# A re-planned attention stage: half as many border copies on GpSimd, one copy tied behind a matmul, and a new order on every engine

## The chip, the cores and the metric

The kernel runs as one program on one core of a Trainium2 chip. A core has five engines, each of which works through its own queue of instructions in order: TensorE (PE in the profile; its weight loads are PEld), VectorE (DVE), ScalarE (ACT), GpSimd (POOL) and SyncE (SP, which here only issues DMAs). An instruction starts when the one before it on its engine has started or ended and when the semaphores that it names have been raised by other engines or by DMAs.

The metric is the device time of one execution in microseconds (us), the median of several runs.

## The reference, cut to what matters

The input is `x` of shape (2, 256, 48, 48): two images (b) of 256 channels. The reference has two layers. Only the first is touched by the change. After a group norm, layer 0 computes a 7x7 local attention with reflected borders and a branch of nine depthwise convolutions, and adds both to the input:

```python
q = (_c1x1(x, Wq, bq) * HD ** (-0.5)).reshape(b * HEAD, HD, n)
k = _c1x1(x, Wk, bk);  v = _c1x1(x, Wv, bv)            # 1x1 convolutions, 4 heads of 64
uk  = _unfold(jnp.pad(k, rpad, mode='reflect'), KA)     # 49 neighbours of each pixel
uv  = _unfold(jnp.pad(v, rpad, mode='reflect'), KA)
upe = _unfold(jnp.pad(pe, rpad[1:], mode='reflect'), KA)
att = softmax(einsum('bdn,bdkn->bnk', q, uk + upe))
out_att = einsum('bnk,bdkn->bdn', att, uv)
...
out_conv = jnp.sum(oc * wts, axis=1)                    # depthwise branch
return rate1 * out_att + rate2 * out_conv
```

Layer 1 (a state space block with a scan, then a mixture of eight experts, two per token) takes the result. Its program is the same before and after.

## The kernel before, in words

The program is three stages, one after the other: layer 0 (to about 315 us of the profile), the state space block (to about 700 us) and the experts (to the end).

**How layer 0 is tiled.** Each image is cut into 18 blocks of 8x16 queries (three blocks make a row of blocks), 36 in all, numbered c = 0 to 35. A block looks at 14x22 = 308 keys. For block c the steps are, with the names that the planner gives them:

- `score` (PE, L810): eight matmuls, queries by keys, for two pairs of heads; into two of three double PSUM banks (`banks`).
- `least` (DVE, L826): mask, and the maximum of each row; `exps` (ACT, L837): exponentials and their sums; `turn` (PE, L845): six transpositions; `copy` (ACT, L851): the transposed probabilities back to SBUF. Each of these exists twice per block, for h = 0 and 1.
- `rden` (DVE, L883): the inverses of the sums; `rx` (POOL, L888): each inverse widened to 64 columns; `rt` (PE, L893): two transpositions that spread the inverses over the output's layout, into the right half of a PSUM bank called `o`; `rc` (ACT, L899): that half copied to SBUF (`rb`).
- `mix` (PE, L867): 24 matmuls, values by probabilities, into the left half of the same bank `o`; `norm` (DVE, L881): left half times `rb`; `add` (DVE, L877): into `x`.

Around the blocks stand steps that serve several of them. `kk` (PE, L702), `ka` (DVE, L708) and `kb` (POOL, L713 to L722) make the keys, in five groups of ten rows (the last of eight) for each image and each h. `kb` mirrors the borders: for j = 0, 1, 2 one column on the left (L715) and one on the right (L717), and in the first and last group three whole rows (L720, L722). `place` (POOL, L691) makes the position term that `ka` adds. `qp` and `q` (PE L659, ACT L667) make the queries of a row of blocks. `v`, `vc`, `vs` (PE L748, ACT L755, a DMA from SP, L758) make the values in 18 pieces; after every three pieces `vt` (SP, L768 to L774, nine DMAs) spreads them into a table in HBM, `ve` (L780, L782) mirrors its ends, and `val` (L910, three DMAs) loads a block's 308 rows of it. The convolution branch is `c1`, `c2`, `c3` on DVE (L565, L577, L603), `cp`, `g2`, `relu` on ACT (L626, L597, L569), and `ca` on POOL (L638), which issues a DMA that adds a product into a sum; `cd` stands for its landing. Lastly there are the statistics of each image (`gs`, `ga`, `rstd`, `xp`), and `winw`, `woutw`, ... which scale weights for layer 1.

**What sets the order.** None of this is written in the order in which it is issued. Every step is declared with an engine, a cost in nanoseconds, what it needs, and what buffers it takes and frees (`op`, class `Flow`). `Flow.run` then plays the declared costs forward: of the steps that are ready, the one with the lowest rank is emitted next on its engine. The rank is a due time (block number times `PACE0`) less the work that still hangs on the step, less an offset for the step's kind from the table `LEAD0`, which has one entry for the first image (`-`) and one for the second (`+`). The emitted order is fixed on PE, DVE, ACT and SP, and chained on POOL. So a changed cost, an added need or a new table reorders the stage on all engines; the chip still waits only on real data and buffers. DMA queues are not modelled as busy: a DMA has only a time from issue to landing.

The buffers that matter: two single PSUM banks (`bank`: shared by `kk`, `qp`, `v` and `o`), three double banks, two `vout`, two `ct`, two `place`, three `val`.

Of the kernel before, what the change touches and what calls it, by code (L numbers as in the profile page):

```python
# [34 lines left out]
ALU = mybir.AluOpType  # L35
# [3 lines left out]
B, C, H, W = 2, 256, 48, 48  # L39
# [3 lines left out]
PAD = 3  # L43
# [189 lines left out]
class Kernel:  # L233
# [133 lines left out]
    def prepare(self, wts):  # L367

        nc, ins, v, r = self.nc, self.ins, self.v, self.r
        l0 = self.l0 = {}  # L370

        def new(name, *shape):
            l0[name] = wts.tile([P, *shape], F32, name=name)
            return l0[name]

        wp = wts.tile([1, 2, P], F32, name="wp")
        pos = wts.tile([1, 2, HP], F32, name="pos")
        line = self.line = wts.tile([P, 2, W], F32, name="line")
        nc.scalar.dma_start(wp, ins["Wp"])
        nc.scalar.dma_start(pos, ins["pos"])  # L380
        for k in ("Wk", "Wq", "Wv"):
            nc.scalar.dma_start(new(k, NH, C), ins[k].rearrange("(h p) o -> p h o", p=P))
        for key, cost in (("cst", 10300), ("vec", 11600), ("row", 14500), ("wp", 9900), ("Wk", 11500), ("Wq", 13500),
                          ("Wv", 15400), ("win", 24200)):
            self.arrival((key, 0), cost)
        vec = nc.vector

        self.op(0, ("bq8", 0), "DVE", 170, lambda: vec.tensor_scalar(
            new("bq8", NH), v["bq"], -(HD ** -0.5), None, ALU.mult), ("vec", 0))
        self.op(0, ("bkp", 0), "DVE", 220, lambda: vec.tensor_scalar(  # L390
            new("bkp", NH), v["bk"], v["bp"], None, ALU.add), ("vec", 0))
        self.op(0, ("w2r", 0), "DVE", 240, lambda: vec.tensor_scalar(
            new("w2r", NH * 9), v["w2"], r["rate2"], None, ALU.mult), ("vec", 0), ("row", 0))

        self.op(0, ("bv1", 0), "DVE", 220, lambda: vec.tensor_scalar(
            new("bv1", NH), v["bv"], r["rate1"], None, ALU.mult), ("vec", 0), ("row", 0))
        self.op(0, ("wv1", 0), "POOL", 1600, lambda: nc.gpsimd.tensor_scalar(
            l0["Wv"], l0["Wv"], r["rate1"], None, ALU.mult), ("row", 0), ("Wv", 0))


        def lines():
            ps = self.bank_for(("line", 0))
            for i in range(2):
                nc.tensor.matmul(
                    ps[:, i * W : (i + 1) * W], lhsT=wp[:, i, :], rhs=pos[:, i, PAD : PAD + W], start=True, stop=True
                )

        self.chain(0, ("line", 0), [
            ("PE", 450, lines),
            ("DVE", 250, lambda: vec.tensor_copy(  # L410
                line.rearrange("p i c -> p (i c)"), self.tiles["bank", ("line", 0)][:, : 2 * W])),
        ], ("wp", 0), takes=[("bank", ("line", 0))], uses=[("bank", ("line", 0))])
# [265 lines left out]
    def keys(self, b, g):  # L678


        nc, l0, T = self.nc, self.l0, self.tiles
        r0, r1 = KG * g, min(KG * (g + 1), H)
        n = (r1 - r0) * W

        c = b * NBQ + NCB * next(rb for rb in range(NRB) if min(QR * rb + QR + PAD, H) > r0)
        old = NCB * (min(NRB - 1, (r1 + PAD - 1 + (PAD if r1 == H else 0)) // QR) + 1) - 1
        rows = slice(PAD + r0, PAD + r1)
# [4 lines left out]
                t, bcast(self.line[:, 0, :], 1, shape), bcast(self.line[:, 1, r0:r1], 2, shape), ALU.add  # L692
            )

        self.op(c, ("place", (b, g)), "POOL", 1100, place, ("line", 0), takes=[("place", (b, g))])
        for h in range(NH):
            key, kp = (b, g, h), self.kp[h]

            def product(h=h, key=key):
                ps = self.bank_for(("kp", key))  # L700
                for k in range(NH):
                    nc.tensor.matmul(  # L702
                        ps[:, :n], lhsT=l0["Wk"][:, k, h * P : (h + 1) * P], rhs=self.xp[b, k][:, r0:r1, :],
                        start=k == 0, stop=k == NH - 1,
                    )

            def add(h=h, key=key, kp=kp):
                nc.vector.scalar_tensor_tensor(  # L708
                    kp[:, rows, PAD : PAD + W], T["bank", ("kp", key)][:, :n].rearrange("p (r c) -> p r c", c=W),
                    l0["bkp"][:, h : h + 1], T["place", (b, g)][:, : r1 - r0, :], ALU.add, ALU.add,  # L710
                )

            def border(kp=kp):  # L713
                for j in range(PAD):
                    nc.gpsimd.tensor_copy(kp[:, rows, j : j + 1], kp[:, rows, 2 * PAD - j : 2 * PAD - j + 1])  # L715
                    lo, hi = PAD + W + j, PAD + W - 2 - j
                    nc.gpsimd.tensor_copy(kp[:, rows, lo : lo + 1], kp[:, rows, hi : hi + 1])  # L717
                for j in range(PAD):
                    if r0 == 0:
                        nc.gpsimd.tensor_copy(kp[:, j, :], kp[:, 2 * PAD - j, :])  # L720
                    if r1 == H:
                        nc.gpsimd.tensor_copy(kp[:, PAD + H + j, :], kp[:, PAD + H - 2 - j, :])  # L722

            self.op(c, ("kk", key), "PE", 4 * 403 * n // 480, product, *self.normalized(b, r0, r1), ("Wk", 0),
                    takes=[("bank", ("kp", key))])
            self.op(c, ("ka", key), "DVE", 700 * n // 480, add, ("kk", key), ("bkp", 0), ("place", (b, g)),
                    *[("score", i) for i in range(old + 1) if b],
                    uses=[("bank", ("kp", key)), ("place", (b, g))])
            self.op(c, ("kb", key), "POOL", 6 * 170 + (3 * 180 if r0 == 0 or r1 == H else 0), border, ("ka", key),
                    ("kb", (b, g - 1, h)) if r1 == H else None)  # L730

    def values(self, b, pair):


        nc, T, p0 = self.nc, self.tiles, 2 * P * pair
        flat = [self.xp[b, h].rearrange("p r c -> p (r c)") for h in range(NH)]
        raster, key = self.vraster[b], (b, pair)
        r1 = (p0 + 2 * P) // W
        done = (p0 + 2 * P) % (VR * W) == 0
        group = p0 // (VR * W)  # L740
        c = b * NBQ + NCB * next(rb for rb in range(NRB) if min(QR * rb + QR + PAD, H) > group * VR)
# [41 lines left out]

        self.op(c, ("v", key), "PE", 1730, product, *self.normalized(b, p0 // W, r1), ("wv1", 0), takes=[("bank", ("v", key))])
        self.op(c, ("vc", key), "ACT", 570, copy, ("v", key), takes=[("vout", key)], uses=[("bank", ("v", key))])
        self.op(c, ("vs", key), "queue", 3700, store, ("vc", key), uses=[("vout", key)])
        if done:
            self.op(c, ("vt", (b, group)), "queue", 10000, spread, *[("vs", (b, p)) for p in range(pair - 2, pair + 1)])
            if group == 0 or r1 == H:
# [2 lines left out]
    def block(self, c):  # L792
# [97 lines left out]
        def spread():  # L890
# [7 lines left out]
        self.op(c, ("rt", c), "PE", 220, spread, ("rx", c), takes=[("bank", ("o", c))], uses=[("rx", c)])  # L898
        self.op(c, ("rc", c), "ACT", 390, lambda: nc.scalar.copy(  # L899
            self.large_tile("rb", c, [P, NH, P]), T["bank", ("o", c)][:, NH * P :].rearrange("p (h q) -> p h q", h=NH)  # L900
        ), ("rt", c), takes=[("rb", c)])
        self.op(c, ("norm", c), "DVE", 430, scale, ("rc", c), ("mix", c), takes=[("ot", c)],
                uses=[("bank", ("o", c)), ("rb", c)])
        self.op(c, ("add", c), "DVE", 390, add, ("norm", c), uses=[("ot", c)])
# [10 lines left out]

    PACE0 = 8517
    LEAD0 = {
        "Wk-": -1119547, "Wq-": -597473, "Wv-": 2514686, "add+": 3062471, "add-": 216523,
        "bkp-": -1357788, "bq8-": -2582335, "bv1-": -2311329, "c1+": -3056772, "c1-": 674391,
        "c2+": -3354012, "c2-": -3259309, "c3+": -4311438, "c3-": -482232, "ca+": 1060332,  # L920
        "ca-": 1695604, "cd+": -4992161, "cd-": 505317, "copy+": 3167330, "copy-": -2132730,
        "cp+": -1186244, "cp-": 185922, "cst-": 1816816, "exps+": -3784293, "exps-": -3837034,
        "g2+": 2518476, "g2-": -2098506, "ga-": -5969754, "gneg-": 1972109, "gs-": -3837384,
        "ka+": -379377, "ka-": 4594388, "kb+": 501331, "kb-": 862328, "kk+": -256854, "kk-":
        105073, "least+": -254337, "least-": -2329953, "line-": -3571457, "mix+": 1625800,
        "mix-": 4892365, "norm+": -2011005, "norm-": -1379637, "place+": 2695259, "place-":
        2798256, "q+": 1131741, "q-": 1346874, "qp+": -260479, "qp-": 44331, "rc+": 1359143,
        "rc-": 555924, "rden+": -3086582, "rden-": -738391, "relu+": 6028778, "relu-": 3311002,
        "row-": -4935504, "rstd-": 5049209, "rt+": -224859, "rt-": -1455, "rx+": -5316670,
        "rx-": -171551, "score+": 2256235, "score-": 1081046, "sw+": -1345634, "turn+": -412799,  # L930
        "turn-": 8318, "v+": 84496, "v-": 32028, "val+": 867987, "val-": 3076092, "vc+": 135346,
        "vc-": -180221, "ve+": 793092, "ve-": -4814757, "vec-": -3443444, "vs+": -1096720,
        "vs-": -3047869, "vt+": 3933614, "vt-": 2501367, "w2r-": -6504385, "win-": 1754314,
        "winw+": -1105244, "woutc+": 705933, "woutd+": 1232417, "woute+": -3991134, "woutt+":
        -1769115, "woutw+": -5095299, "wp-": -2490457, "wv1-": -892855, "x-": -4043795, "xp-":
        -7196893,
    }


# [1485 lines left out]
```

## Time and profile before

| | us |
|---|---|
| runs | 1278.13, 1283.33, 1290.38 |
| median | 1283.33 |
| profiled execution: its own time | 1286.65 |
| its span in the profile | 1284.9 |
| mean granted TensorE clock | 0.979 |
| layer 0: last `add` (DVE, L877) ends | 314.7 |

The span is the stretch from the first to the last instruction of the profiled execution; the device time has 1.75 us around it. In rows of groups, "x" is the number of instructions, then follow busy time and the mean duration of one in ns. A row of waits reads: who waited, for whom, us in total, times, longest. A row of the timeline reads: start, duration, engine, line, operation, and in brackets the idle time ahead of it and what ended it. A row of windows has a stretch's length, then busy time and number of instructions for PE, PEld, DVE, ACT and POOL, the granted clock (1.00 is full speed), and DMA.

### The profile page before, as it was taken

The page shows a single profiled execution, that of the slowest core. Times are in us where ns is not written, and L with a number is a line of the kernel's source. Part 1 is how long each engine was busy: PE and PEld are TensorE (multiplying, and loading weights), DVE is VectorE, ACT ScalarE, POOL GpSimd, SP SyncE. Part 2 cuts the span into 40 slices and gives each one's busy share as a digit, 9 for nine tenths or more (in the row PEclk, how much of TensorE's full clock was granted, in tenths as well). Part 3 has the DMA queues.
Part 4 walks back from the last instruction along what each step waited for, and adds up shares of the span by engine and source line. Part 5 has one row for each costly group of instructions (what it writes and reads, how often), then busy time and mean ns, then how long its engine had stood idle before and what let it go on. Part 6 is the DMA issues. An engine that isn't in the chain of part 4 may idle for free. (4 is left out here: it accounts for less than half of the span.)

```text
span 1284.9 us, 23472 instructions
## 1 busy us (share of the span) xinstructions
PE 1212.2 (94%) x8024; PEld 980.1 (76%) x8024; DVE 895.6 (70%) x2385; ACT 779.3 (61%) x1774; POOL 624.2 (49%) x833
## 2 busy tenths in 40 slices
PE   4889898997899999999999988999999999999995
PEld 2557775776576777777776877999999999999994
DVE  6787897998577977889798644664655565556542
ACT  2479886987889978789697643333333333333342
POOL 4654253523267789999989873112222222212220
PEclk9899998999799999999999998999999999999998
DMA  7598783632223334334545149567667567666756
GB/s 259 137 215 210 187 197 75 149 91 67 70 80 94 89 116 127 112 114 133 176 142 176 58 133 284 178 196 235 229 195 250 179 217 221 234 182 206 229 179 210
DMA packets 106734, 212.99 MB, mean 166 GB/s; under 512 B 11615, under 2 KB 83632, under 8 KB 101680
## 3 DMA queue, kind: packets, MB, share of 16 engines
q1 hardware_dynamic: 85488, 168.51, 38.9%
q0 software_dynamic: 19008, 38.62, 15.8%
q10 hardware_dynamic: 2116, 4.33, 1.0%
q8 instruction: 65, 1.06, 0.3%
q14 instruction: 57, 0.47, 0.1%
HBM read 154.24 MB, written 43.23 MB: 154 GB/s over the span
## 5 line engine op out<-in xcount | busy, mean ns | idle before, releaser
L2153 POOL DMA_INDIRECT acc<-ey,token x70 | 109.3, 1561 | 367.7 <-ACT ey L2152 308.4
L2143 PE MATMUL bank<-ext,wt 128*128 128x256 f32 (+1 forms) x1152 | 241.2, 368 | 0.0
L2147 ACT ACTIVATE hid<-bank,bt 128x256 f32<-128x256 f32 (+1 forms) x288 | 132.0, 460 | 171.3 <-PE bank L2143 166.9
L2143 PEld LDWEIGHTS bank<-ext,wt 128*128 128x128 f32 x1152 | 207.0, 190 | 25.0
L2186 PE MATMUL po<-ts,ss 128*128 128x128 f32 x768 | 96.2, 275 | 0.0
L974 PE MATMUL bank<-xn,win 128*128 128x387 f32 x240 | 92.4, 508 | 2.1 <-ACT t L1057 2.1
L1187 DVE SCALAR_TENSOR_TENSOR xc<-bank,vec,xc 128x384 f32<-128x384 f32 x144 | 86.7, 610 | 8.4 <-ACT xc L1176 8.1
L2186 PEld LDWEIGHTS po<-ts,ss 128*128 128x128 f32 x768 | 90.9, 192 | 0.0
L1403 ACT ACTIVATE mt<-mt,cum 128x128 f32<-128x128 f32 x288 | 87.7, 393 | 0.0
L1737 POOL DMA_INDIRECT xs<-u,rows x72 | 73.2, 1016 | 17.5 <-issue 14.9
L837 ACT ACTIVATE prob<-prob,top 128x308 f32<-128x308 f32 x144 | 78.4, 554 | 1.2 <-DVE top L826 1.2
L2190 ACT COPY u<-po 128x128 f32<-128x128 f32 x32 | 8.5, 265 | 114.0 <-PE po L2186 114.0
L888 POOL COPY rx<-rden 128x256 f32<-128x256 f32 x36 | 36.2, 1049 | 74.1 <-DVE rden L883 56.3
L974 PE MATMUL zbank<-xn,win 128*128 128x384 f32 x192 | 72.0, 497 | 0.0
L1509 PE MATMUL bank<-wout,y 128*128 128x264 f32 x288 | 71.8, 395 | 0.1
L2130 DVE TENSOR_TENSOR ss<-hid 128x512 f32<-128x512 f32 x32 | 22.1, 691 | 70.6 <-ACT hid L2147 70.6
L565 DVE SCALAR_TENSOR_TENSOR hid<-xp,vec,hid 128x1175 f32<-128x1175 f32 (+1 forms) x48 | 69.5, 1452 | 1.0 <-DMA hid<-ct 1.0
L826 DVE CUSTOM_DVE_ANT_0 prob<-banks,cst 128x308 f32<-128x308 f32 x144 | 62.1, 471 | 9.5 <-PE banks L810 9.2
L577 DVE SCALAR_TENSOR_TENSOR x<-hid,w2r,x 128x1128 f32<-128x1128 f32 (+1 forms) x48 | 66.0, 1383 | 0.1
L2186 PE MATMUL po<-wt,hid 128*128 128x128 f32 x496 | 65.5, 275 | 0.0
L845 PE MATMUL banks<-cst,prob 128*112 128x128 f32 x432 | 57.7, 276 | 6.0 <-ACT pt L851 3.9
L1509 PEld LDWEIGHTS bank<-wout,y 128*128 128x128 f32 x288 | 53.7, 194 | 10.1 <-issue 1.1
(340 smaller groups left out, 3015.8 us busy)
## 6 DMA issues: line engine op xcount, KB each, us to landing
wt<-in_We SPq DMA_DIRECT2D x36, 2048.0 KB
mt<-decays SPq DMA_DIRECT2D x36, 512.0 KB
ex<-xs SPq DMA_DIRECT2D x36, 265.0 KB
rd<-decays SPq DMA_DIRECT2D x68, 128.0 KB
val<-vtab SPq DMA_DIRECT2D x72, 112.0 KB
bt<-in_We SPq DMA_DIRECT2D x36, 136.0 KB
hid<-ct POOLq DMA_DIRECT2D x8, 600.0 KB
vraster<-vout SPq DMA_DIRECT2D x18, 256.0 KB
```

What stands on the lines that cost most here:

```text
L565: nc.vector.scalar_tensor_tensor(dst, src, w[:, k : k + 1], dst, ALU.mult, ALU.add)
L577: nc.vector.scalar_tensor_tensor(dst, src, w[:, k : k + 1], dst, ALU.mult, ALU.add)
L837: nc.scalar.activation(t, t, AF.Exp, bias=T["top", c][:, a : a + 1], scale=-1.0, accum_out=T["den", c][:, a : a + 1])
L974: self.nc.tensor.matmul(ps, lhsT=lhs(k), rhs=rhs(k), start=k == 0, stop=k == NH - 1)
L1187: nc.vector.scalar_tensor_tensor(out(), T["bank", ("cv", at)][:, i : i + TB], wc[:, i : i + 1], out(), ALU.mult, ALU.add)
L1403: nc.scalar.activation(t, t, AF.Relu, bias=at_s, scale=-1.0)
L1509: nc.tensor.matmul(ps[:, : C + E], lhsT=T["y", c][:, m, :], rhs=self.l1["wout"][:, m, :], start=m == 0, stop=m == NZ - 1,)
L1737: ins = nc.gpsimd.indirect_dma_start(self.xs, bass.IndirectOffsetOnAxis(ap=of("rows")[:, i, q : q + 1], axis=0), T["u2", g][:, i, :], None,)
L2143: nc.tensor.matmul(ps[:, :rows], lhsT=w1[:, k, c * P : (c + 1) * P], rhs=xt[:, k, :], start=k == 0, stop=k == NH - 1,)
L2147: nc.scalar.activation(hid[:, c, :], ps[:, :rows], AF.Gelu, bias=bt[:, c : c + 1])
L2153: put = nc.gpsimd.indirect_dma_start(self.acc, bass.IndirectOffsetOnAxis(ap=token[:, j : j + 1], axis=0), y, None, compute_op=ALU.add)
L2186: nc.tensor.matmul(p[name], lhsT=v[a][:, c], rhs=v[w][:, c], start=c == 0, stop=c == NHC // 2 - 1)
```

## The change

Five edits, all in layer 0's declarations:

1. `kb` mirrors the left and the right column of one j in one operation with a step of 51 (to) and 43 (from) between the two columns, instead of two operations. Three column operations per `kb` instead of six; there are 20 `kb`.
2. `rc` needs `mix` of its block as well as `rt`.
3. `wv1` (POOL, the value weights times `rate1`) needs `rstd` of the first image.
4. Declared costs: `place` 1260 for 1100, `kb` 1350 (+1200 with rows) for 1020 (+540), `kk` of the first image's first two groups 560 per matmul for 403, `vs` 4500 for 3700.
5. A new table `LEAD0` (all 91 offsets).

```diff
         self.op(0, ("wv1", 0), "POOL", 1600, ...
-            l0["Wv"], l0["Wv"], r["rate1"], None, ALU.mult), ("row", 0), ("Wv", 0))
+            l0["Wv"], l0["Wv"], r["rate1"], None, ALU.mult), ("row", 0), ("Wv", 0), ("rstd", 0))
...
-        self.op(c, ("place", (b, g)), "POOL", 1100, place, ...
+        self.op(c, ("place", (b, g)), "POOL", 1260, place, ...
...
             def border(kp=kp):
                 for j in range(PAD):
-                    nc.gpsimd.tensor_copy(kp[:, rows, j : j + 1], kp[:, rows, 2 * PAD - j : 2 * PAD - j + 1])
-                    lo, hi = PAD + W + j, PAD + W - 2 - j
-                    nc.gpsimd.tensor_copy(kp[:, rows, lo : lo + 1], kp[:, rows, hi : hi + 1])
+                    to, of = PAD + W, W - 2 - PAD
+                    nc.gpsimd.tensor_copy(
+                        kp[:, rows, j : j + to + 1 : to], kp[:, rows, 2 * PAD - j : 2 * PAD - j + of + 1 : of]
+                    )
...
-            self.op(c, ("kk", key), "PE", 4 * 403 * n // 480, product, ...
+            self.op(c, ("kk", key), "PE", 4 * (403 if b or g > 1 else 560) * n // 480, product, ...
-            self.op(c, ("kb", key), "POOL", 6 * 170 + (3 * 180 if r0 == 0 or r1 == H else 0), border, ...
+            self.op(c, ("kb", key), "POOL", 3 * 450 + (3 * 400 if r0 == 0 or r1 == H else 0), border, ...
...
-        self.op(c, ("vs", key), "queue", 3700, store, ...
+        self.op(c, ("vs", key), "queue", 4500, store, ...
...
         self.op(c, ("rc", c), "ACT", 390, ...
-        ), ("rt", c), takes=[("rb", c)])
+        ), ("rt", c), ("mix", c), takes=[("rb", c)])
...
     LEAD0 = {
-        "Wk-": -1119547, "Wq-": -597473, "Wv-": 2514686, "add+": 3062471, "add-": 216523,
+        "Wk-": -2983844, "Wq-": -2364428, "Wv-": 1379269, "add+": 4672699, "add-": -218998,
...
```

What the new order is, as the built programs have it: on PE, both `kk` of the fourth key group move ahead of the first queries, and the second row's queries (`qp`) move from before the second and third `score` to behind the third; the second image's statistics (`rstd`) move up to just behind the first `score`. On DVE, that image's statistics and `xp` likewise move up. On POOL, the four `winw` and four `woutw` move up among the first blocks, and for the second image `rx` 16 and 17 move ahead of most of the `kb`. On SP, the second `vt` moves from behind the first three `val` to ahead of them, and the second image's value pieces come earlier. From block 18 on the two orders differ mostly by a place or two. Every step of the state space block and the experts is emitted in the same order as before.

More of the change, by code (lines that the diff above doesn't have):

```diff
@@ L693, in place @@
             )
-        self.op(c, ("place", (b, g)), "POOL", 1100, place, ("line", 0), takes=[("place", (b, g))])
+        self.op(c, ("place", (b, g)), "POOL", 1260, place, ("line", 0), takes=[("place", (b, g))])
         for h in range(NH):
@@ L722, in border @@
                         nc.gpsimd.tensor_copy(kp[:, PAD + H + j, :], kp[:, PAD + H - 2 - j, :])
-            self.op(c, ("kk", key), "PE", 4 * 403 * n // 480, product, *self.normalized(b, r0, r1), ("Wk", 0),
+            self.op(c, ("kk", key), "PE", 4 * (403 if b or g > 1 else 560) * n // 480, product, *self.normalized(b, r0, r1), ("Wk", 0),
                     takes=[("bank", ("kp", key))])
@@ L728, in keys @@
                     uses=[("bank", ("kp", key)), ("place", (b, g))])
-            self.op(c, ("kb", key), "POOL", 6 * 170 + (3 * 180 if r0 == 0 or r1 == H else 0), border, ("ka", key),
+            self.op(c, ("kb", key), "POOL", 3 * 450 + (3 * 400 if r0 == 0 or r1 == H else 0), border, ("ka", key),
                     ("kb", (b, g - 1, h)) if r1 == H else None)
@@ L785, in values @@
         self.op(c, ("vc", key), "ACT", 570, copy, ("v", key), takes=[("vout", key)], uses=[("bank", ("v", key))])
-        self.op(c, ("vs", key), "queue", 3700, store, ("vc", key), uses=[("vout", key)])
+        self.op(c, ("vs", key), "queue", 4500, store, ("vc", key), uses=[("vout", key)])
         if done:
@@ L917 @@
     LEAD0 = {
-        "Wk-": -1119547, "Wq-": -597473, "Wv-": 2514686, "add+": 3062471, "add-": 216523,
[L919 to L935, printed above, removed]
@@ L936 @@
-        -7196893,
+        "Wk-": -2983844, "Wq-": -2364428, "Wv-": 1379269, "add+": 4672699, "add-": -218998,
+        "bkp-": -329119, "bq8-": -347513, "bv1-": -2824447, "c1+": -2744499, "c1-": 604148,
+        "c2+": -3568598, "c2-": -4067744, "c3+": -4192745, "c3-": 1206176, "ca+": -316981,
+        "ca-": 1533923, "cd+": -6915146, "cd-": 3124390, "copy+": 5626139, "copy-": -1580149,
+        "cp+": -1382670, "cp-": -1157911, "cst-": 2506359, "exps+": -3895413, "exps-": -4687265,
+        "g2+": 3892042, "g2-": -3058028, "ga-": -6766507, "gneg-": 557252, "gs-": -9485502,
@@ new lines @@
+        "ka+": -2261356, "ka-": 4495797, "kb+": 754107, "kb-": 2128455, "kk+": -355426, "kk-":
+        95965, "least+": -852851, "least-": -3615547, "line-": -4892590, "mix+": 3379755,
+        "mix-": 5352508, "norm+": -2808328, "norm-": -848702, "place+": 2730989, "place-":
+        4548299, "q+": 272749, "q-": 1258423, "qp+": -359879, "qp-": 5581, "rc+": -1347439,
+        "rc-": 1599623, "rden+": -1647488, "rden-": -463776, "relu+": 7308982, "relu-": 4577314,
+        "row-": -5624948, "rstd-": 3924930, "rt+": 965921, "rt-": -18691, "rx+": -6558515,
@@ new lines @@
+        "rx-": -3369941, "score+": 3504231, "score-": 2190083, "sw+": -848532, "turn+":
+        -1205935, "turn-": 84883, "v+": 110806, "v-": 10811, "val+": 448065, "val-": 3685159,
+        "vc+": -519738, "vc-": -124400, "ve+": 2263088, "ve-": -7064210, "vec-": -4450165,
+        "vs+": -1985565, "vs-": -5738649, "vt+": 5333280, "vt-": 1460046, "w2r-": -7510221,
+        "win-": 4743570, "winw+": -1186160, "woutc+": 774295, "woutd+": 1826874, "woute+":
+        -6026117, "woutt+": -512791, "woutw+": -8672401, "wp-": -1208524, "wv1-": -2064644,
@@ L937 @@
+        "x-": -4900900, "xp-": -8007513,
     }
```

## The prediction

> **What bounds the kernel now.** Only layer 0 can change; every later step keeps its order. I read the page's forty slices first, then windows over layer 0, its waits, and the timeline of the worst places.
>
> The slices are 32 us each, layer 0 the first ten:
>
> ```profile
> PE   4889898997899999999999988999999999999995
> DVE  6787897998577977889798644664655565556542
> ACT  2479886987889978789697643333333333333342
> PEclk9899998999799999999999998999999999999998
> ```
>
> TensorE and VectorE share the load; a stage with two engines at 8 or 9 tenths gains only where both idle. The windows show where (us from the start; PE busy is the second number):
>
> ```profile
> 40.00:60.00 20.00, 14.21 (x49) 7.54 (x48) 12.52 (x31) 7.69 (x22) 12.49 (x29) 0.83 0.67 151
> 80.00:106.00 26.00, 20.91 (x145) 14.74 (x145) 13.46 (x31) 20.87 (x49) 11.03 (x11) 1.00 0.93 218
> 190.00:206.00 16.00, 12.93 (x66) 8.11 (x64) 10.90 (x18) 7.89 (x14) 8.21 (x10) 0.79 0.48 108
> 206.00:300.00 94.00, 90.87 (x765) 64.52 (x762) 86.36 (x215) 85.17 (x199) 37.11 (x69) 1.00 0.47 105
> ```
>
> PE idles 5.8, 5.1, 3.1 and 3.1 us there, 14 of 17 us in three places; the first and third also run at a cut clock. From 206 on PE is busy for 97%: nothing to win.
>
> The waits in layer 0 (who, for whom, us, times, longest):
>
> ```profile
> ACT rb L899 <- PE bank L867: 19.1, 13, 5.7
> ACT ct L626 <- DMA hid<-ct: 12.8, 3, 11.0
> PEld bank L867 <- ACT rb L899: 6.3, 8, 1.9
> PE bank L748 <- ACT q L667: 6.1, 2, 5.8
> PE bank L659 <- ACT vout L755: 3.1, 1, 3.1
> PE bank L893 <- POOL rx L888: 3.1, 1, 3.1
> ```
>
> One wait each makes the holes. The first, from the timeline:
>
> ```profile
> 33.43 6.03 DVE L565 SCALAR_TENSOR_TENSOR hid<-xp,vec,hid 128x1175 f32<-128x1175 f32 x4
> 35.40 1.41 POOL L717 COPY kp<-kp 128x10 f32<-128x10 f32 x1
> 41.40 0.21 POOL L717 COPY kp<-kp 128x10 f32<-128x10 f32 x1
> 45.80 1.07 POOL L638 DMA_DIRECT2D hid<-ct  x1
> 51.48 1.29 ACT L626 ACTIVATE ct<-xp,vec 128x1200 f32<-128x1200 f32 x1 [11.00 <-DMA hid<-ct]
> 54.37 3.78 PE L748 MATMUL bank<-Wv,xp 128*128 128x256 f32 x8 [5.79 <-ACT q L667]
> ```
>
> A border copy takes 0.20 us alone and about 1.4 beside a VectorE tap. Eighteen of them, seven blocked, fill POOL until 45.8, and the sum's DMA stands behind them; ScalarE waits 11 us for its landing, TensorE for ScalarE. The second hole is a value store queued on SP behind `val` loads: ScalarE waits 4.2 us for `vout`, PE 3.1. The third is `rx` 17 behind border copies.
>
> **My measure: lag.** A step's lag is its start less all PE work ahead of it in its program. Prices are start to start in the timeline: `kk` 1.6 (3.2 for the first four), `v` 1.62, `qp` 1.30, `score` 1.10, `turn` 0.65, `mix` 1.48, `rt` 0.30; 253 us in both orders. Before: score 0 starts at 41.4 with 26.0 ahead, lag 15.4; first `turn` 61.7 − 37.0 = 24.7; mix 2 89.6 − 60.7 = 28.9; mix 3 103.1 − 69.8 = 33.3; score 8 114.8 − 80.0 = 34.8; score 17 42.5; score 18 200.0 − 152.4 = 47.6; score 35 57.9. A smaller lag at the same place is time won, if VectorE follows.
>
> **The change, part by part.**
>
> *Paired columns.* Groups L715 and L717 are 60 copies each, 25.3 and 21.7 us busy, mean 438 and 376 ns. Sixty paired ones take their place. A pair has 20 elements per partition; the nearest rows are 10 elements in 0.20 and 54 contiguous ones in 0.23, so 0.22 alone and, as before, the rest of a tap when blocked. [...]by the rows 0.21 to 0.22: the fixed part is what is saved. Free price: 120 × 0.20 − 60 × 0.22 = 11 us of POOL; at most half of the 47 busy. Nothing of it counts until someone waits for POOL. Bounds: zero to the two holes above. If a pair cost as much as two singles the gain would be nil.
>
> *First hole.* In the new order the sixth tap of the first sum comes at a VectorE position 2 us earlier, and nine copies, not 18, stand ahead of its DMA: the `ca` at about 39.5 instead of 45.8. It lands 5.6 us later (45.8 to 51.4 before), at 45, when ScalarE reaches it. What is late next: PE goes through two more `kk` and a `v` to the end of score 0 at 45.7, then meets the second image's statistics, now third behind it. Their last VectorE step has 37.7 us of VectorE work ahead, 4.0 more than the first `least` had (33.7, at 45.0): 49.0. PE waits 3.3. Then `v`, score 1, statistics, and the first `turn` at 52.5 with 33.6 ahead: lag 18.9, 5.8 less than before.
>
> *Value table on SP.* The second `vt`, nine issues, moves ahead of the first three `val`, and every `val` and value store waits behind it. It waits for its third store (ScalarE reaches that `vc` at about 57 by the same sums on its queue; landed 61.3, with the 4 us that `vout` waited); nine issues took 5.5 us at 40 to 46, but 9.6 at 75.9 to 85.5. With 5.5 the first `val` is issued by 69, and lands near 72. `mix` 0 would be due at about 68 (18.9 + 47.5, and 1.4 of small waits for `exps`): a new PE wait of about 4, and VectorE's `norm` 0, its queue behind, also stands 4. Bounds 3 to 9; I take 4, the nearest row being the first `vt`, on as quiet a DMA. Lag at mix 0: 72 − 47.5 = 24.5 (before 25.9).
>
> *Second hole.* After `mix` 0 the stores of pieces 6 to 8 are waited on by one `val` at most. Going on by the same prices: mix 2 at 86.1 with 60.7 ahead (lag 25.4), mix 3 at 91.1 with 65.7 (25.4), score 8 at 103 with 77.0 (26). Before it was 34.8: 8.8 us won. VectorE's queue is at lag 27.5 there against 33.0: 5.5 won. I take 7 of both. `winw` and `woutw` on POOL (about 2 and 1.6 us each) go ahead of `rx` 1 and 3, which the new order needs 13 and 2 us later: nothing, and up to 2 us if taps block them.
>
> *Clock.* The two new PE waits are 3.3 and 4 us. [...] In the trace 5.8 us of idle gave the 0.83 row and 3.1 the 0.79 row, but another gap of 3.1 stayed at 1.00. [...]nothing net.
>
> *`rc` behind `mix`.* The trace has this wait already, 13 times and 19.1 us, since both halves share a bank; where the copy came first, `mix` waited for it (PEld 6.3 us, PE 2.7). The new order puts the copy where ScalarE need not stand. ScalarE is not last from 106 on, so I book 0; at most the 2.7, and minus 2 if `norm`, waiting for a later copy, holds its bank longer.
>
> *Third hole.* `rx` 17 now precedes most `kb`, which removes PE's 3.1. What is late next: score 18 has only four `qp` (5.2 us) between it and the last `kk` it needs; `place` 2.2 and three blocked pairs 4.2 follow that: it waits about 3, where the old path lost 4.9. Gain 1.5; bounds minus 3 and 4.
>
> *Rest.* `wv1` stood behind `rstd` on POOL already: 0. The costs act only through the order. From block 18 on the orders differ by a place or two, under 97% load: 0, within 2 either way.
>
> Sum: 7 + 1.5 = 8.5. The profiled execution is 1286.65 (span 1284.9 and 1.75 around it), 3.3 above the median; it would become 1278, the median 1275.
>
> **The rivals.**
> 1. *More is won (0.22).* VectorE follows TensorE fully (8.8), the third hole closes (4), and no clock cut returns (2): 15 us, 1268. For it: ScalarE's 19 us vanish too. Against: two new PE waits.
> 2. *Nothing (0.15).* The pair is blocked as long as two, and what PE wins early it waits out at VectorE, whose work is as large: 1283. Against: VectorE idles 12.5 of 26 us in the second hole.
> 3. *Slower (0.10): `vt` in front of the first `val`.* At 9.6 us of issue and a landing of 4, `mix` 0 starts at 77 (5 worse than my sum), the longer gap cuts the clock (3.4), and pieces 6 to 8, on SP behind a `val` that waits for `mix` 0, hold `vout` again (4.2), 13 in all: 8.5 won becomes 4.5 lost, 1288. It decides once the first `val` lands after about 78. For it: SP's `val` issues stood 94 us behind `mix` before; against: SP is quiet at 60.
>
> **How the numbers follow.** My forecast has 0.53, within 1270 to 1281 by the bounds above; the range reaches from between rival 1 and its far end to near rival 3: 1264 to 1286. About 1%, 12.8 us, is what a measurement of this kernel can tell from none. Faster by over 1%: rival 1 and a little of mine, 0.26. Slower: a third of rival 3 and unknowns, 0.06. The rest 0.68.
>
> **What would show it.** Right: copies L716 (60) near 0.22 us when free; ScalarE's 11 us wait for the sum's DMA gone; the first `turn` at about 52 to 53; PE waiting some 4 us for `val` ahead of `mix` 0; score 8 near 103; no wait of `rb` on L867-like matmuls above 2 us in all; last `add` near 306. Wrong: score 18 waiting over 6 us, or `mix` 0 beyond 77.

## The result, and the profile after

The changed kernel takes 1276.45 us, median of 18 runs (1272.95 to 1280.27), against 1281.70 us for the kernel before in the same runs (18, 1275.74 to 1290.38). The ratio is 0.9964, 95% interval 0.9947 to 0.9980: about 4.6 us won, where the forecast won 8.5. A second set, in the experiments below, gave 0.9953 (0.9937 to 0.9970), 6.0 us. In what follows a hundredth of ratio is turned into 12.8 us, and the changed kernel stands at the mean of the two sets, 0.9958.

The profiled execution has a span of 1273.9 us (own time 1275.69). Its slices, on nearly the same scale as before, 31.8 us each:

```profile
PE   4989999997999999999999989999999999999995
DVE  7966899997687988888888645655555655556442
ACT  2488887997889888789698633333333333334342
PEclk9989999998899999999999999999999999999998
```

Within layer 0 the second and the seventh slice had a cut clock before (8 tenths); now it is the third. TensorE's 8 there is all that is left of its weak early slices. The windows over layer 0 (start to end, length, PE, PEld, DVE, ACT and POOL busy with their instructions, clock, DMA share, GB/s); the single row is of the kernel before, the rows below it are of the changed one:

```profile
60.00:80.00 20.00, 19.98 (x138) 14.62 (x139) 19.26 (x44) 17.76 (x23) 12.79 (x25) 1.00 0.74 182
```

```profile
40.00:60.00 20.00, 19.07 (x91) 12.24 (x90) 18.27 (x47) 9.91 (x21) 12.39 (x15) 1.00 0.80 196
60.00:80.00 20.00, 14.87 (x71) 9.34 (x70) 12.78 (x20) 14.94 (x25) 14.25 (x20) 0.83 0.87 216
80.00:106.00 26.00, 26.00 (x217) 19.98 (x216) 18.14 (x50) 24.47 (x53) 11.25 (x13) 1.00 0.76 192
106.00:150.00 44.00, 40.90 (x315) 31.27 (x314) 36.20 (x76) 38.58 (x86) 6.47 (x10) 1.00 0.81 205
190.00:206.00 16.00, 14.05 (x52) 6.30 (x48) 15.38 (x29) 10.63 (x22) 11.53 (x19) 1.00 0.45 93
206.00:300.00 94.00, 93.64 (x838) 70.13 (x838) 90.61 (x224) 90.18 (x213) 35.56 (x50) 1.00 0.51 114
```

The holes at 40 to 60 and at 80 to 106 are filled (14.21 to 19.07, 20.91 to 26.00). A new one has opened at 60 to 80: 19.98 to 14.87, with the clock at 0.83. The stage from 206 on, which I had called full at 90.87, went to 93.64. The waits of layer 0 (who, for whom, us, times, longest):

```profile
DVE ot L882 <- ACT rb L900: 11.8, 9, 4.7
ACT vout L756 <- DMA vraster<-vout: 10.3, 3, 4.2
ACT rb L900 <- PE bank L868: 7.0, 6, 4.6
PE bank L868 <- DMA val<-vtab: 3.4, 1, 3.4
```

ScalarE's 12.8 us for the first sums' DMAs are gone but for 1.0. Its 19.1 us of `rb` waiting for the value product are 7.0, and 4.6 of these stand at block 0, whose `mix` itself waits for `val`. In their place ScalarE waits 10.3 us for value stores (4.2 before), TensorE waits for `val`, and VectorE's `norm` waits 11.8 us for the copy (6.8 before), 4.7 of them again at block 0. The timeline has the places (start, busy us, engine, line, operation, then the wait before it); the first `val` is from the same view of SP's queue:

```profile
41.00 1.10 POOL L638 DMA_DIRECT2D hid<-ct  x1
46.81 1.30 ACT L626 ACTIVATE ct<-xp,vec 128x1200 f32<-128x1200 f32 x1 [0.23 <-DMA hid<-ct]
52.52 0.84 PE L846 MATMUL banks<-cst,prob 128*112 128x128 f32 x6
58.82 0.58 ACT L756 COPY vout<-bank 128x512 f32<-128x512 f32 x1 [2.46 <-DMA vraster<-vout]
68.51 10.02 SPq L911 DMA_DIRECT2D val<-vtab  x12
73.65 2.83 PE L868 MATMUL bank<-pt,val 84*64 84x128 f32 x24 [3.40 <-DMA val<-vtab]
115.86 0.58 ACT L756 COPY vout<-bank 128x512 f32<-128x512 f32 x1 [3.63 <-DMA vraster<-vout]
152.43 0.58 ACT L756 COPY vout<-bank 128x512 f32<-128x512 f32 x1 [4.21 <-DMA vraster<-vout]
```

In lags (start less the PE work ahead, before to after): first `turn` 24.7 to 18.8, `mix` 0 25.9 to 26.2, score 8 34.8 to 30.4, score 17 42.5 to 42.0, score 18 47.6 to 43.4, score 35 57.9 to 49.6. So the win of the first hole is lost at `mix` 0, 4.4 us are there again at score 8, nearly all of that is gone at score 17, and what remains at the end arises from score 18 on. The last `add` starts at 305.1 instead of 314.3. The spans differ by 11.0 us, the medians only by about 5: the profiled execution of before was one of its slower ones (1286.65 against a median of 1281.70).

### The profile page after: what moved, and what is told of

It is laid out like the page before. It is cut to its first block, busy times and chain, and to the rows that moved or that the text cites. A ratio compares the mean times of both kernels' runs of the same rounds, so it can differ in the third digit from the quotient of the medians.

```text
span 1273.9 us, 23367 instructions
## 1 busy us (share of the span) xinstructions
PE 1205.9 (95%) x8024; PEld 977.0 (77%) x8024; DVE 897.5 (70%) x2385; ACT 779.9 (61%) x1774; POOL 612.7 (48%) x773
## 5 line engine op out<-in xcount | busy, mean ns | idle before, releaser
L2131 DVE TENSOR_TENSOR ss<-hid 128x512 f32<-128x512 f32 x32 | 22.1, 691 | 70.6 <-ACT hid L2148 70.6
L1510 PE MATMUL bank<-wout,y 128*128 128x264 f32 x288 | 70.3, 389 | 0.1
L889 POOL COPY rx<-rden 128x256 f32<-128x256 f32 x36 | 30.8, 858 | 70.9 <-DVE rden L884 59.2
L975 PEld LDWEIGHTS bank<-xn,win 128*128 128x128 f32 x240 | 42.6, 196 | 24.4 <-issue 4.2
```

The source lines that it names most:

```text
L975: self.nc.tensor.matmul(ps, lhsT=lhs(k), rhs=rhs(k), start=k == 0, stop=k == NH - 1)
L1510: nc.tensor.matmul(ps[:, : C + E], lhsT=T["y", c][:, m, :], rhs=self.l1["wout"][:, m, :], start=m == 0, stop=m == NZ - 1,)
```

## The experiments

Each kernel computes the whole result. They ran in three sets, each beside the kernel before, whose median was 1281.47, 1278.92 and 1284.17 us there; ratios are to it, and kernels of different sets are compared by their ratios.

### Each half of the change alone, and the change again

The paired copies in the old program:

```diff
-  kp[:, rows, j : j+1] <- column 2*PAD-j ; kp[:, rows, lo : lo+1] <- column hi     (two copies)
+  kp[:, rows, j : j + to + 1 : to] <- columns 2*PAD-j and 2*PAD-j+of             (one copy)
```

> The kernel before with only the paired column copies; order, costs and offsets untouched. Theory A (POOL's queue ahead of the first sum's DMA is a part of the gain): nine pairs stand there instead of eighteen copies, the first ca is issued at 39.5 to 42 instead of 45.8, ScalarE's 11.0 us wait for its landing falls below 7, the first turn comes at 56 to 59 instead of 61.7, and the copies' free price stays near 0.22 us; the whole is 1 to 4 us faster than before. Theory B (the new order brings all of it): the time is that of before within 1 us, because the second hole, at 83 to 103, takes back what the first gives.

Measured: 1274.82 us, ratio 0.9951 (0.9938 to 0.9963). From its timeline:

```profile
39.25 1.10 POOL L638 DMA_DIRECT2D hid<-ct  x1
45.86 1.30 ACT L626 ACTIVATE ct<-xp,vec 128x1200 f32<-128x1200 f32 x1 [5.80 <-DMA hid<-ct]
86.17 0.59 ACT L756 COPY vout<-bank 128x512 f32<-128x512 f32 x1 [4.53 <-DMA vraster<-vout]
```

The first sum's DMA leaves 6.5 us earlier, ScalarE waits 5.8 us for it instead of 11.0, and the first `turn` is at 53.8 with a lag of 16.7, 8.0 better. The store's wait in the second hole is still there. Unlike in the changed kernel, the win stays: 7.1 us at score 8 and at score 17, 9.0 at score 18. Theory A had the place right and the amount too low, since 6.3 us is above its 1 to 4; theory B falls.

The order without the pairs, that is the changed kernel with the single copies:

```diff
-  one copy of two columns (stride PAD + W)
+  two copies of one column each
```

> The changed kernel with the 120 single column copies put back; its order is untouched. Theory A: the copies ahead of the first ca double, it is issued at 43 to 45 instead of 41.0, the first turn moves to 55 or 56, and score 18 waits 3 to 5 us for its border copies instead of 1.2: 1 to 4 us slower than the changed kernel, some 1278 to 1280. Theory B: the order carries the gain, the time is that of the changed kernel within 1 us.

Measured: 1282.66 us, ratio 1.0021 (1.0006 to 1.0036), no gain at all. Its timeline answers the lines above:

```profile
44.88 1.10 POOL L638 DMA_DIRECT2D hid<-ct  x1
51.01 1.29 ACT L626 ACTIVATE ct<-xp,vec 128x1200 f32<-128x1200 f32 x1 [5.35 <-DMA hid<-ct]
205.76 0.89 PE L810 MATMUL banks<-kp,q 64*128 64x308 f32 x2 [2.96 <-POOL kp L715]
```

The first `turn` comes at 58.7, and score 18 waits for its copies in two places (1.28 at 202.0 and 2.96 here) instead of 1.16 in all. Theory A's places are right, its amount is again too low: 8 us above the changed kernel (1282.66 against 1274.64, run side by side).

> The changed kernel once more, timed beside the others, with a second profile. If the 9.5 us by which layer 0 ended earlier in the two profiles is the change, layer 0 ends at 305 (within 1) again[...]. The time should be 4 to 5 us below the kernel before.

Measured: 1274.64 us, ratio 0.9953; in its profile the last `add` starts at 306.0, so layer 0's end belongs to the change and is not a chance of one profile. The kernel before has only one profile, so how far its 314.3 varies stays open; the program after layer 0, the same in all these kernels, took 965 to 972 us.

Pairs alone won as much as the whole change (0.9951 against 0.9958), the order alone won nothing. So the order is worth nothing in sum: it does nothing, or it holds a gain and a loss.

### The value stores

A third `vout` buffer in the changed kernel. Its memory is that of a small operand read once at the start; the order is untouched.

```diff
+  slot = number of vout tiles so far % 3          (was: one of 2)
-  wp = wts.tile([1, 2, P], ...)
+  wp = self.m.tile([P, 2, C], ..., tag="vout2")[:1, :, :P]
```

> The changed kernel with a third vout buffer (its memory is that of wp, which is read once at the start); order untouched. Theory A (the value stores, late on SP, took back the early win between blocks 8 and 17): ScalarE's 10.3 us of waits for stores go to under 2, with TensorE's 2.3 and 3.1 and the half clock at 154; score 17 comes with a lag of 36 to 38 instead of 42.0, and 4 to 6 us are left at the end, some 1271. Theory B (from block 10 on the engines are full, and any stall ahead is soaked up): score 17 keeps a lag over 40.5, and the time is that of the changed kernel within 1.5 us.

Measured: 1267.43 us, ratio 0.9908 (0.9891 to 0.9925), 7.2 us by the medians and 5.8 by the ratios below the changed kernel run beside it. Of ScalarE's 10.3 us of waits for stores none is left. Two windows of it:

```profile
60.00:80.00 20.00, 17.41 (x102) 11.93 (x104) 17.30 (x30) 17.20 (x39) 19.54 (x20) 1.00 0.90 219
106.00:150.00 44.00, 42.90 (x369) 33.33 (x368) 41.41 (x89) 42.27 (x96) 9.30 (x13) 1.00 0.85 221
```

Between 106 and 150 TensorE does 42.90 us instead of 40.90, VectorE 41.41 instead of 36.20: the engines were not full there. The lag is 23.7 at score 8 and 28.6 at score 17, where the changed kernel had 30.4 and 42.0. Theory A's place is right; part of it lies where I had not looked, ahead of `mix` 0, which starts at 68.2: the store that the second `vt` waits for no longer stands behind a `vout` wait (2.46 us in the changed kernel), and the `val` lands earlier. This profiled execution is the fastest of seven (1260.1 span), 5.2 us ahead of the next, so its lags flatter; the medians are the measure.

The third buffer with the pairs in the old order:

```diff
   (kernel before, paired copies)
+  third vout buffer as above
```

> The kernel before, in its own order, with the paired copies and the third vout buffer. Theory A (the order is worth nothing; the two causes are POOL's queue and the stores): ScalarE's wait of 4.5 us and TensorE's of 3.3 for vout at 86 are gone, score 8 has a lag of 22 to 24 instead of 27.7, and the time is 1267 to 1270, as with the third buffer in the new order. Theory B (the new order is better once the stores are out of the way): 1271 or more.

Measured: 1268.80 us, ratio 0.9924 (0.9905 to 0.9943); the wait at 86 is gone, score 8 has a lag of 22.1. Theory A holds: with pairs and third buffer the two orders differ by 0.0016, within the two intervals. In the old order the buffer is worth 3.5 us (the intervals of the two ratios just overlap).

### The second value table ahead of the first `val`

In the changed kernel, nine DMA issues are moved back behind nine others on SP:

```diff
   vt(0,1) in the queue:
-  vt(0,1)  val 0  val 1  val 2
+  val 0  val 1  val 2  vt(0,1)
```

> The changed kernel with the second vt issued right behind the first three val on SP instead of right ahead of them; all else is in place. Theory A ([...]the late stores take the win back anyway): mix 0 starts at 69 to 70 instead of 73, without its 3.4 us wait for val and without the cut of the clock at 72; score 8 has a lag of 24 to 26 instead of 29 or 30; score 17 has 40 or more again, and the time is that of the changed kernel within 1.5 us. Theory B (a win at block 0 stays): score 17 at 37 to 38, some 1270.

Measured: 1266.87 us, ratio 0.9906 (0.9887 to 0.9925), about 6.7 us below the changed kernel. From its timeline:

```profile
70.43 1.54 PE L874 MATMUL bank<-pt,val 84*64 84x128 f32 x24
110.05 0.59 ACT L756 COPY vout<-bank 128x512 f32<-128x512 f32 x1 [3.58 <-DMA vraster<-vout]
149.66 0.59 ACT L756 COPY vout<-bank 128x512 f32<-128x512 f32 x1 [5.06 <-DMA vraster<-vout]
```

`mix` 0 starts without a wait and takes 1.54 us instead of 2.83, for the clock is not cut (1.00 from 60 to 80, against 0.83); score 8 has a lag of 24.5 instead of 30.4. The store waits come again, and at score 17 the lag is 39.1: of 5.9 us half is lost, half stays. Both theories were part right, and B's time was nearer; it is better than I allowed either. In the profile layer 0 ends at 302.7 instead of 305.6 and 306.4, so 3 to 4 of the 6.7 us show there; this execution, at 1269.98, is one of the two slowest of six.

Both mended together:

```diff
+  third vout buffer
+  vt(0,1) behind val 0, 1 and 2
```

> The changed kernel with the third vout buffer and the second vt behind the first three val, both. Theory A (each wait ahead of mix 0 counts once the stores no longer hold): mix 0 starts at 66 to 67 instead of 68.2, and the time is 1 to 3 us below the third buffer alone, some 1265. Theory B (soaked up later, by work that is full): that of the third buffer alone, 1267, within 1 us.

Measured: 1260.94 us (four runs, 1259.79 to 1261.32), ratio 0.9857 (0.9836 to 0.9879). This is the best kernel of the study, 18 us below before and about 13 below the changed one. `mix` 0 starts at 67.5, the clock is 1.00 in every window of layer 0 up to 206 and 0.99 from 206 to 300, score 17 has a lag of 28.9. One store wait of 1.2 us is left. By the medians the two mends add up: theory A, and more than it said. Where the moved `vt` wins its 6.5 us beside the third buffer is not shown: layer 0 ends at 294.0 here and at 293.7 in the profile with the buffer alone, which is that kernel's fastest run. The old order, which has the first three `val` ahead anyway, stood at 0.9924 with pairs and third buffer. Against that kernel the mended new order wins 8.6 us, so the new order does hold a gain.

### The place of `rc`

In the changed kernel each `rc` goes to ScalarE right behind its `rt`, ahead of `mix`, where an `rb` buffer is free:

```diff
   emitted with rt (PE):
+  rc (ACT), if one of the two rb is free
   emitted after mix:
-  rc (ACT)
```

> The changed kernel with each rc issued on ScalarE right behind its rt, ahead of mix, wherever one of the two rb buffers is free by then. Theory A (my zero for rc behind mix): ScalarE's waits of rb for the value product come back, and the time stays that of the changed kernel within 1.5 us. Theory B (those 19 us of waits counted): 3 to 5 us slower, some 1278 to 1280.

Measured: 1280.36 us, ratio 1.0011 (0.9999 to 1.0022), 6.8 us slower than the changed kernel. From its waits, then its windows, between 206 and 300:

```profile
PEld bank L869 <- ACT rb L906: 4.5, 8, 0.8
PE bank L869 <- ACT rb L906: 2.7, 6, 0.6
```

```profile
206.00:300.00 94.00, 89.60 (x778) 65.28 (x775) 87.02 (x217) 86.12 (x199) 33.15 (x51) 1.00 0.50 112
```

The value product waits for the copy, in bits of up to 0.8 us, and TensorE does 89.60 us of work there, near the kernel before (90.87), not 93.64. From score 19 to score 35 the lag grows by 9.2 us; before it was 8.8, in the changed kernel 4.5. So the place of this copy can make or unmake the gain of the last stage, which I had put at nothing. The time is that of theory B and a little above; the way is neither theory's, for ScalarE's waits for the value product do not come back. The kernel before waited differently in the same stretch:

```profile
ACT rb L899 <- PE bank L867: 5.1, 5, 1.6
PEld bank L867 <- ACT rb L899: 0.8, 1, 0.8
PE bank L867 <- ACT rb L899: 0.6, 1, 0.6
```

There 20 of 36 copies stood ahead of `mix`, here all 36 do. So 6.8 us is the price of the early place everywhere; how much of the way from before to changed the copy makes is not shown. The opposite edit, in the old order:

```diff
   emitted with rt, 20 of 36 times ahead of mix:
-  rc (ACT)
   emitted with mix (PE):
+  rc (ACT)
```

> The kernel before, in its own order and with its single copies, with one thing: each of the 20 rc that stand ahead of their mix in the program is issued on ScalarE right behind it. Theory A (the place of rc is worth 4 to 6 us in any order): 1274 to 1278 where before has 1280 or so, and the lag from score 18 to score 35 grows by about 6 instead of 10.3. Theory B (it is worth that only in the new order, where a rc ahead of mix comes more often): within 1.5 us of the kernel before.

> The kernel before in its own order with the paired copies and each rc behind its mix. Theory A: 4 to 6 us below the pairs alone, some 1269 to 1271, which beats the changed kernel, for the old order has the first three val ahead of the second vt. Theory B: that of the pairs alone, 1273 to 1275.

> The kernel before in its own order with the paired copies, the third vout buffer and each rc behind its mix. Theory A (apart from the place of rc and of the second vt the new order is worth nothing): within 3 us of the changed kernel with the third buffer and the first val ahead, 1261 to 1264. Theory B (the new order has more in it): 1266 or more.

Measured: alone 1290.04 us, ratio 1.0060 (1.0037 to 1.0083); with the pairs 1282.80, 0.9991 (0.9976 to 1.0007); with pairs and third buffer 1278.41, 0.9968 (0.9955 to 0.9981). Each is slower than the same kernel without it, by 7.7, 5.1 and 5.6 us. In the first two both theories fall: A would gain, B would stay, and it loses. In the third the time is in B's range, 1266 or more, but it comes from the same loss. The first one's waits, 206 to 300:

```profile
ACT rb L904 <- PE bank L867: 14.2, 10, 4.3
DVE ot L884 <- ACT rb L904: 3.5, 6, 1.3
```

In the kernel before the same two were 5.1 us in 5 and 1.4 in 3; in the changed kernel, `rc` behind `mix` throughout, ScalarE does not wait for the value product there at all. In these three kernels the copy is queued as `mix` is, so ScalarE stands until `mix` has ended, with the exponentials of the next blocks queued behind. The changed kernel's planner emits the copy only once `mix` has ended by its declared cost, and other ScalarE work stands between: its copies in this stretch start up to 2.5 us after `mix` ends. The planner with the added need and the old table was not run, so need and table are not parted. The last of the three has all that the best kernel has (pairs, third buffer, first `val` ahead, `rc` behind `mix`) except the new order itself, and is 14 us behind it (0.9968 against 0.9857). But 5.6 of these are what the late copy costs in the old order; the other 8.6 are the gain found above. The place of `rc` has a part in it, at 6.8 us if the early place everywhere is the measure; which other places of the new order share in it is open.

### Whether the pairs still count when the rest is mended

```diff
   (changed kernel, third vout, val first)
-  one copy of two columns
+  two copies of one column each
```

> The changed kernel with the third vout buffer and the first three val ahead of the second vt, and the single column copies in place of the pairs. Theory A (POOL's queue ahead of the first sum's DMA and of score 18 sets the pace whatever else is mended): 5 to 8 us slower than the same with pairs, 1266 to 1269; first turn at 57 to 59, and TensorE waiting 3 us or more at score 18. Theory B (with the other stalls gone the later stages have the slack to take it up): within 2 us of 1261.

Measured: 1277.67 us, ratio 0.9951 (0.9934 to 0.9968): 12.0 us slower than with pairs, above theory A's 5 to 8. From its timeline:

```profile
49.90 1.29 ACT L629 ACTIVATE ct<-xp,vec 128x1200 f32<-128x1200 f32 x1 [5.24 <-DMA hid<-ct]
194.51 0.80 PE L819 MATMUL banks<-kp,q 64*128 64x308 f32 x4 [1.28 <-POOL kp L718]
198.25 1.40 PE L819 MATMUL banks<-kp,q 64*128 64x308 f32 x4 [2.94 <-POOL kp L718]
```

5.1 us at the first `turn` (57.4 against 52.3); 7.8 by score 18 (194.5 against 186.7); 11.9 by score 19, for the clock is 0.79 from 190 to 206 (1.00 with pairs), and behind the wait of 2.94 four `kk` matmuls take 3.56 us at 199.6 instead of 1.88 with pairs. With everything else out of the way POOL's queue sets two places by itself.

## Why the prediction was right or wrong

The forecast of 1275 missed the median by 1.5 us, and the change lies within 1% of no change, as the likeliest case had it. That it came so near is luck in part: its sum was too large by 2.5 to 4 us, the kernel before ran 1.6 us below the median it started from, and its terms were off by more, with both signs. The pairs bring 6.3 us alone and 8 in the new order. The order brings next to nothing, because it holds both signs: a gain of about 9 us (against the old order, both with pairs, third buffer and first `val` ahead), in which the place of `rc` has a part that was not measured by itself, and losses of about 7 (`vt` ahead of `val`) and 6 (stores, of which the old order with pairs has 3.5 too), 13 when both are mended. Each part was measured by undoing it, so the parts overlap and don't add exactly.

- **Paired columns: right.** Sixty copies, 0.202 / 0.218 / 1.54 us shortest, median, longest, against 0.202 for a single one; 0.22 was said. A pair costs what the rows of the profile said, not the price of two copies.
- **First hole: right, in part by luck.** The `ca` at 41.0 (39.7 in the second profile; 39.5 said), ScalarE waits 0.23 us, first `turn` with its weight load at 52.4 (52.5), lag 18.8 (18.9). But it came from the pairs, not from the order to which I gave 2 us of it: the old order with pairs issues the `ca` at 39.25, the new order without them at 44.88. And the wait of 3.3 us at the second image's statistics did not come: TensorE ended score 0 at 48.9, 3.2 later than said, and found them ready.
- **Value table on SP: mechanism right, term mis-sized.** A wait of 4 was said, 3.4 came, but from 70.3 to 73.65 and not from 68 to 72: the first `val` left at 68.5 (69) and landed 1.7 later than said. Nothing net was booked for the clock, an estimate that set it off against what the old hole paid (4.9 us at 0.50 behind its wait, 54.4 to 59.2), when 5.5 us at 0.50 lay behind this wait (73.65 to 79.1), some 2.7 lost (an estimate, half of it). Lag at score 8: 26 said, 30.4 measured; the late landing and the clock make the 4.4. With the table behind it is 24.5. The price of this place was about 7 us of the median.
- **Second hole: failed step.** "Going on by the same prices" up to score 8 and leaving the lag alone from there assumed that no store would be late again. The new order queued `vs` behind `val`, `ve` and a `vt` at 115 and 152 and held `vout` for 3.6 and 4.2 us; the third buffer showed what that is worth. I had read the stores for pieces 6 to 8 of the first image and not those of the second.
- **`rc` behind `mix`: failed step.** Zero was booked, with bounds -2 and +2.7; with every copy early again it costs 6.8, which is more than undoing. "ScalarE is not last from 106 on" was an average. In the kernel with early copies the waits that count are TensorE's own, in bits under a microsecond that a list of longest waits hides. The sign that no wait of `rb` above 2 us in all would be left did not come either: 7.0 are left, 4.6 of them from the late `val`.
- **Third hole: sign right.** Of the 4.2 won at score 18, 3.7 arise behind score 17, where 1.5 was said; score 18 waited 1.2, not 3, and no cut of the clock followed (1.00 from 190 to 206), as one had at 195.8 to 202.6 before (0.50). Here my upper bound of 4 was nearly the value.
- **Rest: failed step.** "Busy for 97%: nothing to win" took three missing per cent of 94 us for nothing; they are 3 us, and 2.8 of them came.
- **The rivals.** The third has its mechanism confirmed, `vt` ahead of `val`, the clock (0.83 from 60 to 80, 3.4 us short of full), then `vout` held, though by stores of the second image and not of pieces 6 to 8; it did not decide because `mix` 0 came at 73.65, not 77, and because the order won elsewhere. The second's claim that the pairs gain nothing falls. The first's evidence, ScalarE's vanished 19 us, pointed at the step that I had put at nothing, but how much of the gain those waits make is not shown.

## What to carry to other kernels

A reordered program is a bundle: undo its parts one at a time, since a gain of 9 and losses of as much show in the sum as nothing. For each DMA queue follow every store and its buffer through the whole stage, not just the next one. An instruction that must wait for another engine is cheap only if its own engine has other work queued ahead of it: the copy behind `mix` cost 5 to 8 us where it was queued too early.

## What the runs showed of the hardware

The clock granted in one stretch of a program differs between its executions. In the changed kernel's first profile PE's 3.40 us wait for `val` ended at 73.65, and the clock was at 0.50 from 72.3 to 79.1, so 5.5 us of half clock lay behind the wait. TensorE has work throughout (busy 5.46 us of it), so half of that is lost: 2.7 us, an estimate. From 60 to 80 that profile is 3.4 us short of full clock (0.83 of 20 us); the second is about 1.8 us short (0.91):

```profile
60.00:80.00 20.00, 14.59 (x75) 9.08 (x75) 12.69 (x19) 15.34 (x28) 14.21 (x20) 0.91 0.88 208
```

The five cuts within layer 0 in the first profile of the changed kernel and in that of the kernel before, all to 0.50, lasted 6.8 us (from 52.4 and 195.8 before, from 72.3 changed) or 3.4 us (from 151.4 before, from 154.2 changed).

The length of a wait does not order the waits with and without a cut. In the kernel before a wait of 1.91 us was followed by a cut (the granted clock is the third number from the right), while the one of 3.1 us at 91.9 to 95.0 was not (1.00 from 80 to 106).

```profile
150.27 0.87 PE L845 MATMUL banks<-cst,prob 128*112 128x128 f32 x6 [1.91 <-ACT pt L851]
144.00:152.00 8.00, 6.09 (x64) 5.15 (x63) 8.00 (x11) 6.54 (x10) 2.41 (x2) 0.96 0.69 154
152.00:160.00 8.00, 8.00 (x71) 6.14 (x68) 5.18 (x17) 7.21 (x17) 1.70 (x2) 0.82 0.94 237
```

In the changed kernel a wait of 2.28 us, at 114.9 to 117.2, was not followed by one, and the wait of 3.1 us that ended at 153.2 was:

```profile
112.00:120.00 8.00, 5.17 (x41) 3.69 (x41) 4.44 (x9) 4.37 (x13) 1.25 (x2) 1.00 0.73 201
120.00:128.00 8.00, 7.73 (x75) 6.38 (x72) 8.00 (x14) 8.00 (x18) 0.40 (x1) 1.00 0.60 181
152.00:160.00 8.00, 6.84 (x54) 5.45 (x56) 5.66 (x16) 7.37 (x19) 2.35 (x3) 0.79 0.81 197
```

So the length of a wait alone does not tell whether the clock is cut; what else decides is open.
